# Four layers on 16 images of 28 x 28: one tile for all padded signs, and another order of VectorE's and ScalarE's steps where one layer ends and the next begins

## The chip, the cores and the metric

The kernel runs on one core of one Trainium2 chip. The metric is the device time of one execution in microseconds (us); for the kernel before it is 963.3 us, the median of three runs (963.19 to 964.45). TensorE is called PE in the profile, VectorE DVE, ScalarE ACT, GpSimd POOL and SyncE SP.

## What is computed

The input is a tensor of 16 images, 256 channels, 28 x 28 pixels, in fp32. Four layers follow each other:

```python
# layer 0: signs, 3x3 convolution with signs of weights, batch norm, residual
y = sat_conv2d(sign(x), sign(w)) * mean(abs(w));  x = bn_over_batch(y) * gamma + beta + x
# layer 1: per image, two branches with a squeeze-and-excite gate each
residual = prelu(x, a_alpha1)
y = prelu(bn(conv3x3(hardsign(x + a_move), clip(a_w))), a_alpha2)
y = bn(gate(mean(s * x + (1 - s) * y)) * y * residual) + residual
u = prelu(bn(conv1x1(hardsign(y + f_move), clip(f_w))), f_alpha2)
x = bn(gate(mean(s2 * y + (1 - s2) * u)) * u) + y
# layer 2: norm over the batch, signs, binary convolution, twice; norm; residual
o = prelu(binconv(sign(batchnorm(x)), w1), a1)
o = prelu(binconv(sign(batchnorm(o)), w2), a2)
x = prelu(batchnorm(o) + x, a3)
# layer 3: attention over the 784 pixels of an image, width 64
q, k, v = Wq x, Wk x, Wv x;  x = Wp softmax(q k / 8) v + x
```

The norms of layers 0 and 2 are over all images. So the next layer can't begin before the last image's statistics are there: these places are called borders here.

## The kernel before, in words

The channels lie on the 128 partitions in two groups (k = 0, 1). An image is 784 columns, and a matmul takes half of them (HN = 392), one bank of PSUM.

**Layer 0 and the two halves of layer 2** are `sign_layer` (L330 on). Its list of blocks says what is worked on at a time. For layer 0 the list is `whole_images(PARTS)`: IMAGES (L52) are taken whole, and the rest of PARTS follows: image 15 as one half and two quarters. For every block `products` issues the matmuls of L348 (18 for a half image, all into one tile of two PSUM banks), ScalarE writes the signs of the next image into `fpads`, `post` issues VectorE's statistics of the block before (L616, L1180), one or two weight steps follow, and `apart` splits the packed sums: ScalarE twice (L359, L360), VectorE once (L362). `fpads` is a tile for two images with a border of zeros, which POOL clears (`sign_pads`, L109). It is made once for layers 0 (in the space that layer 1 uses for `vs`) and once more for layer 2. Layer 1 has two such tiles of its own, `pads` (L493), which POOL clears in `constants` (L561).

**Border 0 to 1.** `norm` (L189) makes scale and shift from the statistics. ScalarE computes the two shifts (L213), `zb1` and `bi0`, in a row; `enter` (L685, VectorE) and `sign1` (L693, ScalarE) make image 0's signs, `transform` (L698, VectorE) the sums that the convolution L732 takes.

**Layer 1** is `iteration(b)` for 15 images, written so that the steps of three images interleave, and `last_iteration` for image 15. Its two convolution results of one parity are `conv_pair` with i = 0, 1: the two banks of one tile, read by `rows_out` (L771, VectorE, L777). After it, from L1060, come the last gates and the statistics for layer 2: `squares` (L883, ScalarE), `products` (L886, VectorE; both write a scrap tile "rn" of two buffers), `unit_u` (L865, ScalarE), `unit_b` (VectorE), the small steps L1079 to L1101, `gates`, a table load for the square root (L1105) and `sign_norm`. `keep_busy(n)` (L437) issues n matmuls on a tile of zeros whose result is not used.

**Border to attention.** After layer 2 `norm("l2c", ...)` gives `sg3` and `bg3` by VectorE alone, a dummy exponential loads its table (L1229), and `attend_unshifted` begins: for each half of image 0, `finish_a` (ScalarE: scale and shift, L1345), `finish_b` (VectorE: add and prelu, L1353 and L1354), `queries_keys` (PE, L1367). Then queries and keys are copied out of PSUM (L1374, L1378) and the scores (L1390) begin.

**The end.** For the last image the denominators (L1411) are inverted (L1437), watched by ScalarE (L1612, L1615), the values copied (L1617) and multiplied (L1441), projected (L1471) and added (L1480, L1482), and stored in two parts from ScalarE's queue (L1503). `raise_flag` (L1495) sums up the watched numbers and sets `flag`, which every engine loads at the end (L1258) to decide whether a careful second run of all is needed.

Within `tc.manual_schedule(engines=...)` the named engines run their instructions in the order of the program; outside it a scheduler orders them. Waits are set by the framework from the tiles that are read and written.

Of the kernel before, what the change touches and what calls it, by code (L numbers as in the profile page):

```python
# [27 lines left out]
F32 = mybir.dt.float32  # L28
# [22 lines left out]
NB = len(PARTS)  # L51
IMAGES = [(i, 0, S) for i in range(B - 1)]  # L52
EARLY = 22
# [30 lines left out]
def forward(ctx: ExitStack, tc: tile.TileContext, d: dict, out: bass.AP, careful: bool):  # L84
# [24 lines left out]
    def sign_pads(pool, tag):  # L109

        t = pool.tile([P, 2, 2, S + 2, S + 2], SIGNS, tag=tag, name="fpads")
        for i in (0, S + 1):
            for edge in (t[:, :, :, i:i + 1, :], t[:, :, :, :, i:i + 1]):
                nc.gpsimd.memset(edge.bitcast(F32) if careful else edge, 0.0)
        return t
# [72 lines left out]

    def norm(name, moments, gamma, beta, sf=None, then=lambda r: None, shifts=()):  # L189


        half, e = vtile(name + "_half"), vtile(name + "_e")
        V.tensor_scalar(half, gamma, -0.5, None, ALU.mult)
        if sf is not None:

            tt(e, sf, sf, ALU.mult)
            V.tensor_scalar(e, e, 1e-30, 1.0 / EPS, ALU.max, ALU.mult)
            V.reciprocal(e, e)
        m, var = moments()
        v, c, less = vtile(name + "_v"), vtile(name + "_c"), vtile(name + "_less") if shifts else None  # L200
        if sf is not None:
            tt(v, var, e, ALU.add)
        else:
            V.tensor_scalar(v, var, EPS, None, ALU.add)
        r = rsqrt(name, v, half, (lambda: V.tensor_scalar(less, m, -1.0, None, ALU.mult)) if shifts else None)
        then(r)
        if not shifts:
            tt(c, m, r, ALU.mult)
            return r, tt(c, beta, c, ALU.subtract)
        cs = [vtile(f"{name}_c{i}") for i in range(len(shifts))]  # L210
        for o, b in zip(cs, shifts):
            for k in range(2):
                A.activation(o[:, k:k + 1], r[:, k:k + 1], AF.Identity, bias=b[:, k:k + 1], scale=less[:, k:k + 1])  # L213
        return r, *cs

# [213 lines left out]
    with tc.tile_pool(name="ps_conv", bufs=3, space=PSUM) as psc, \  # L429
# [13 lines left out]
        with tc.tile_pool(name="ph1", bufs=1) as ph:  # L443

            fpads = sign_pads(ph, "vs")
            xs, ns = [None] * B, [None] * B
# [45 lines left out]

            pads = [const.tile([P, 2, S + 2, S + 2], BF16, tag=f"pad{i}", name=f"pad{i}") for i in range(2)]  # L493

# [60 lines left out]

            moved = vtile("moved")

            def constants():
                tt(moved, pv("b0"), pv("a_move"), ALU.add)
                for p in pads:  # L560
                    nc.gpsimd.memset(p, 0.0)  # L561
# [9 lines left out]
                for i, bn in enumerate(bns):  # L571
# [3 lines left out]
                    tt(c_bn[:, two], bn[:, 1::4], c_bn[:, two], ALU.subtract)  # L575
                tt(cc, c2, c4, ALU.add)

                for o, q in ((ra1, "a_alpha1"), (ra2, "a_alpha2"), (rf2, "f_alpha2")):
# [166 lines left out]
            def conv_pair(b, mo, i, u, parts=range(2)):  # L745
                if i == 0 and 0 in parts:
                    pairs[b, mo, u > 0 and u < 3] = conv_ps()
                conv(b, mo, u, pairs[b, mo, u > 0 and u < 3][:, i, :HN], parts)

            def first_pair():  # L750
                ps = pairs[0, 0, True] = conv_ps()
                for part in range(2):
                    for i, u in enumerate((1, 2)):
                        conv(0, 0, u, ps[:, i, :HN], (part,))
# [8 lines left out]
            def sum_pair_b(b, mo):  # L763
# [5 lines left out]
                pairs[b, mo] = uv  # L769

            def rows_out(b, mo, rows=range(2)):  # L771
                ps, uv = pairs[b, mo, False], pairs[b, mo]
                if 0 in rows:
                    ys[b, mo] = full("yu", f"y{b}_{mo}", 6)
                two = ys[b, mo].rearrange("p (a two b) -> p two a b", two=2, b=S)
                for i in rows:
                    V.scalar_tensor_tensor(  # L777
                        two[:, i], ps[:, i, :HN].rearrange("p (a b) -> p a b", b=S), us1[:, mo:mo + 1],
                        uv[:, i].rearrange("p (a b) -> p a b", b=S), ALU.mult, ALU.add,
                    )  # L780
# [195 lines left out]
            def last_iteration(b):  # L976
# [32 lines left out]
                px = hidden_x(B, TWO)  # L1009
                conv_pair(b, 1, 0, 0, (0,))  # L1010
                h = hidden_a(B, px, TWO)
                sum_pair_b(b, 1)
                h = hidden_b(B, h, TWO)
                conv_pair(b, 1, 0, 0, (1,))
                rows_out(b, 1, (0,))
                g = gates(h, some=TWO)
                conv_pair(b, 1, 1, 3)
                branch2(b - 1, 0, g[:, 1])
# [14 lines left out]
            with tc.manual_schedule(engines={ET.PE, ET.DVE, ET.Activation}):  # L1033
                sc0, zb1, bi0 = norm("l0", mom, pv("g0"), pv("b0"), sf0, first, (moved, pv("b0")))
                mom.doubt(doubts[:, 0:2 * NB])
                sign1(0, 0)
                enter(0, 1, sc0)
                sign1(0, 1)
                for k in range(2):
                    for u in (1, 2):  # L1040
                        transform(0, u, k)
# [31 lines left out]
                squares(x2[b][:, 0, :], shift[:, 0:1], sum_vv[:, 0:1])  # L1073
                for i, v in ((b, sum_vv[:, 1:2]), (b - 1, sum_sq[:, 1, b - 1:b])):
                    products(x2[i][:, 1, :], shift[:, 1:2], x2[i][:, 1, :], v)

                last = wpool.tile([P, 2, N], F32, tag="wa", name="last")
                px = hidden_x(B + 1, TWO)
                V.tensor_reduce(m1, sum_x2[:, :, 0:B - 1], AX.X, ALU.add)  # L1079
                tt(m1, m1, sv, ALU.add)  # L1080
                V.scalar_tensor_tensor(without_g[:, 0], m1, 1.0 / (B * N), shift, ALU.mult, ALU.add)
                unit_u(b, 0, last[:, 0, :])
                unit_b(b, 0)
                tt(d1, sv, sum_x2[:, :, b - 1], ALU.add)
                V.scalar_tensor_tensor(d1, shift, 2.0 * N, d1, ALU.mult, ALU.add)
                V.scalar_tensor_tensor(
                    sum_vv[:, 1:2], d1[:, 1:2], shift[:, 1:2], sum_vv[:, 1:2], ALU.mult, ALU.add
                )
                unit_u(b, 1, last[:, 1, :])
                unit_b(b, 1)  # L1090
# [3 lines left out]
                h = hidden_b(B + 1, hidden_a(B + 1, px, TWO), TWO)  # L1094
                for k in range(2):
                    products(x2[b][:, k, :], shift[:, k:k + 1], us[b, k], sum_uv[:, k:k + 1])
                V.tensor_scalar(of_g[:, 0], su, 1.0 / (B * N), None, ALU.mult)
                V.tensor_scalar(without_g[:, 1], sum_uv, 2.0 / (B * N), None, ALU.mult)
                V.tensor_reduce(v1, sum_sq[:, :, 0:B - 1], AX.X, ALU.add)
                tt(v1, v1, sum_vv, ALU.add)  # L1100
                V.tensor_scalar(v1, v1, 1.0 / (B * N), EPS, ALU.mult, ALU.add)  # L1101
                g = gates(h, dqg[:, 2], TWO)
                keep_busy(14)

# [21 lines left out]
        with tc.tile_pool(name="ph2", bufs=1) as ph:  # L1126
            if careful:
                w2b = packed_weights(ph, tag="wb")
            fpads = sign_pads(ph, "fpads")

# [93 lines left out]

            keep_busy(45)
            sg3, bg3 = norm("l2c", mom, pv("g3"), pv("b3"), sf2)
            tt(bg3, bg3, cc, ALU.add)

            A.activation(small.tile([P, 2], F32, tag="mv", name="e"), sg3, AF.Exp, scale=0.0)  # L1229

# [70 lines left out]
def attend_unshifted(ctx, tc, d, out, wqk, wv, wp, keys, worst, doubts, flag, pv, finish):  # L1301
# [126 lines left out]
    def denominators(b):  # L1428

        dns[b] = two_banks(pssc, "sc")[:, 0, :HN] if b == B - 1 else one_bank(pssm, "sm")  # L1430

# [76 lines left out]
    with tc.manual_schedule(engines={ET.PE, ET.Activation, ET.DVE, ET.Pool}):  # L1508

        ps = [two_banks(psmi, "mi"), two_banks(pssc, "sc")]  # L1510
        for h in range(2):
            n = slice(h * HN, h * HN + HN)
            finish_a(0, n)
            finish_b(0, n)
            queries_keys(0, h, ps[h])
        keep_busy(8)
        for h in range(2):
# [83 lines left out]
        for c in range(3):  # L1601
            values(b, c)
        denominators(b)
        for c in range(3, NC_):
# [6 lines left out]
        junk = buf("junk", 1, shape=(P, HN))  # L1611
        A.activation(junk, dns[b], AF.Copy, accum_out=watched[0])  # L1612
        for n in parts:
            invert(b, n)
        A.activation(junk[:, parts[0]], r[:, parts[0]], AF.Copy, accum_out=watched[1])  # L1615
        V.tensor_reduce(watched[2], r[:, parts[1]], AX.X, ALU.add)
        A.copy(os[b][0], avs[b][:, :HN])  # L1617
        up = raise_flag(two_banks(psmi, "mi")[:, 0, :])
        for n in parts:
            normalize(b, n)  # L1620
        up()

# [4 lines left out]
                (parts[1], 0, [one_bank(pssm, "sm"), one_bank(psav, "av")]),  # L1627
                (parts[1], 1, two_banks(pssc, "sc")),
            )
        ]  # L1630
        for add in adds[0::2]:
            add()
        store(b, slice(0, 1), nc.scalar)
        for add in adds[1::2]:
            add()
# [179 lines left out]
```

## Time and profile before

| | |
|---|---|
| device time, median of 3 (lowest, highest) | 963.3 us (963.19, 964.45) |
| profiled execution: its own time, its span | 963.05 us, 961.3 us |
| mean granted TensorE clock | 0.998 |
| layer 0, last real matmul ends | about 107.7 us |
| layer 1, first matmul | 114.95 us |
| layer 2, first matmul of its two halves | 468.52, 573.68 us |
| first scores of the attention | 686.83 us |
| last store issued, end | about 956, 961.3 us |
| DMA, mean | 110 GB/s |

All times are from the start of the span. The profile gives, for each engine, when an instruction began and how long it took, and for idle time what ended it. The chain that ended last is followed back from the last instruction through what released each step. An average share of busy time says little here; the borders are short and have limits of their own, so they are read in the timeline.

### The profile page before, as it was taken

How to read it: one execution, taken by the hardware profiler on the slowest of the kernel's cores; microseconds unless marked ns; L12 is line 12 of the kernel's file. 1: busy time of each engine (PE TensorE's matmuls, PEld its weight loads, DVE VectorE, ACT ScalarE, POOL GpSimd, SP SyncE). 2: the span in 40 equal slices, each digit the busy share in tenths (PEclk: the TensorE clock that was granted, in tenths of full speed). 3: DMA queues.
4: the chain of work that ended last, by engine and by line, in shares of the span. 5: the costliest groups of instructions: out<-in, count | busy, mean ns of one | idle time of the engine just before them, and what ended most of it. 6: DMA issues, size and time to landing. Idle time of an engine off the chain costs nothing.

```text
span 961.3 us, 14808 instructions
## 1 busy us (share of the span) xinstructions
PE 942.2 (98%) x5613; PEld 578.4 (60%) x5619; DVE 773.4 (80%) x1424; ACT 719.0 (75%) x1200; POOL 140.9 (15%) x149
## 2 busy tenths in 40 slices
PE   8999999999999999999999999999999999999995
PEld 4555577787778778776555555555444444444442
DVE  3777798999988888977799988999666868777765
ACT  6887768888887888865788868888666666676652
POOL 3001100000000000000100000000145353444431
PEclk9999999999999999999999999999999999999999
DMA  9978512444433233101670000000043443425212
GB/s 344 347 272 287 198 34 84 147 141 149 146 103 101 101 134 110 42 35 67 239 297 1 1 1 2 1 1 1 14 81 75 89 114 79 123 72 131 67 68 105
DMA packets 26948, 105.82 MB, mean 110 GB/s; under 512 B 3490, under 2 KB 7268, under 8 KB 26868
## 3 DMA queue, kind: packets, MB, share of 16 engines
q1 hardware_dynamic: 20948, 73.44, 21.5%
q0 software_dynamic: 5632, 30.54, 11.7%
q8 instruction: 46, 0.75, 0.3%
q10 hardware_dynamic: 288, 0.80, 0.2%
q14 instruction: 34, 0.28, 0.1%
HBM read 72.67 MB, written 32.11 MB: 109 GB/s over the span
## 4 chain that ended last, share of the span: by engine, by line
PE 84%; DVE 9%; ACT 3%; issue 1%; DMA 1%; SPq 1%; DVEq 0%; ACTq 0%
PE cv L732 29%; PE cv L348 22%; PE sc L1390 8%; PE av L1411 8%; PE cv L852 4%; PE mi L1367 4%; DVE p L1178 2%; PE sm L1453 2%; PE mi L1471 2%; PE sm L1411 1%; DVE ab L362 1%; DMA xs<-in_x_dram 1%; DVE l2c_fin L1180 1%; DVE l2b_fin L1180 1%; PE hid L642 1%
## 5 line engine op out<-in xcount | busy, mean ns | idle before, releaser
L348 PE MATMUL cv<-fpads,wpk 128*128 128x392 f16 (+1 forms) x1746 | 295.3, 331 | 2.1 <-DVE wpk L275 1.1
L732 PE MATMUL cv<-vs,w 128*128 128x392 bf16 (+1 forms) x1536 | 285.8, 355 | 1.8 <-DVE vs L134 1.4
L348 PEld LDWEIGHTS <-wpk 128*128 128x128 f16 x1746 | 169.3, 97 | 128.7 <-issue 3.0
L732 PEld LDWEIGHTS cv<-vs,w 128*128 128x128 f32 x768 | 142.0, 190 | 10.7
L1394 ACT ACTIVATE es<-sc 128x784 f32<-128x784 f32 x112 | 87.3, 822 | 41.4 <-PE sc L1390 41.4
L732 PEld LDWEIGHTS <-w 128*128 128x128 f16 x768 | 66.3, 99 | 56.7 <-issue 17.7
L1390 PE MATMUL sc<-q,keyswa 64*128 64x392 f32 x448 | 89.9, 513 | 0.9 <-ACT es L1394 0.9
L359 ACT ACTIVATE t<-cv,rounding 128x392 f32<-128x392 f32 (+2 forms) x82 | 51.9, 633 | 41.4 <-PE cv L348 41.4
L1178 DVE SCALAR_TENSOR_TENSOR p<-ab,vec 128x392 f32<-128x392 f32 x128 | 79.1, 618 | 2.3
L1411 PE MATMUL av<-es,v 128*64 128x392 f32 x448 | 80.7, 499 | 0.0
L1404 POOL TENSOR_TENSOR sum<-sum,es 128x784 f32<-128x784 f32 x32 | 67.2, 2100 | 3.1 <-ACT es L1394 0.7
L1390 PEld LDWEIGHTS sc<-q,keyswa 64*128 64x128 f32 x448 | 38.9, 186 | 44.0 <-issue 17.1
L1378 DVE COPY keyswa<-mi 64x392 f32<-64x392 f32 x31 | 16.3, 565 | 52.7 <-ACT q L1374 52.7
L880 POOL DMA_DIRECT2D x2d<-x x16 | 8.6, 537 | 336.7 <-DVE x L874 276.1
L1411 PEld LDWEIGHTS av<-es,v 128*64 128x64 f32 x448 | 29.4, 136 | 47.4 <-issue 47.0
L714 ACT CAST vs<-vs 128x840 fp32r<-128x840 bf16 x63 | 54.1, 883 | 2.9 <-DVE vs L134 2.9
L852 PE MATMUL cv<-z,fw 128*128 128x392 f32 x256 | 48.6, 341 | 0.1
L362 DVE SCALAR_TENSOR_TENSOR ab<-ab,cv 128x392 f32<-128x392 f32 x64 | 35.4, 553 | 16.4 <-ACT ab L360 16.4
L852 PEld LDWEIGHTS cv<-z,fw 128*128 128x128 f32 x256 | 45.9, 188 | 1.0 <-ACT z L844 0.9
L1367 PE MATMUL mi<-p,wqk 128*128 128x392 f32 x124 | 45.1, 506 | 0.1
L1402 POOL TENSOR_TENSOR sum<-es 128x784 f32<-128x784 f32 x16 | 30.0, 1876 | 91.0 <-ACT es L1394 91.0
L441 PE MATMUL unused<-idle 128*128 128x512 bf16 x166 | 39.6, 394 | 3.2 <-POOL idle L477 3.0
(290 smaller groups left out, 1502.9 us busy)
## 6 DMA issues: line engine op xcount, KB each, us to landing
xs<-in_x_dram SPq DMA_DIRECT2D x30, 784.0 KB, 5.9
x2d<-x POOLq DMA_DIRECT2D x16, 784.0 KB, 3.6
out_dram<-p SPq DMA_DIRECT2D x15, 784.0 KB, 3.7
p<-x2d POOLq DMA_DIRECT2D x14, 784.0 KB, 6.8
p<-x2d SPq DMA_DIRECT2D x13, 784.0 KB, 15.3
n0d<-n POOLq DMA_DIRECT2D x16, 392.0 KB, 5.6
n<-n0d SPq DMA_DIRECT2D x16, 392.0 KB, 3.2
st<-in_w_dram SPq DMA_DIRECT2D x12, 384.0 KB, 6.5
```

Of the source, the lines that this page charges most:

```text
L348: T.matmul(pss[j][:, n // size if careful else h, :rows * S].rearrange("p (a b) -> p a b", b=S), lhsT=w[:, n, t, :], rhs=pads[:, blocks[j] ...
L359: A.activation(by_halves(t, blocks[j]), ps, AF.Identity, bias=rounding, scale=1.0 / PACK)
L362: V.scalar_tensor_tensor(a, b, -PACK, ps, ALU.mult, ALU.add)
L714: copy(v, w)
L732: T.matmul(ps.rearrange("p (a b) -> p a b", b=S), lhsT=w[:, k, c, u, mo * P:(mo + 1) * P], rhs=v[:, b % 2, u, k, :, c:c + S], start=((part ...
L852: T.matmul(ps[:, h, :HN], lhsT=w[:, k, mo * P:(mo + 1) * P], rhs=z2[b][:, k, h * HN:(h + 1) * HN], start=(k + i == 0), stop=(k + i == 2),)
L1178: V.scalar_tensor_tensor(p, y, alpha[:, mo:mo + 1], y, ALU.mult, ALU.max)
L1367: T.matmul(ps[:, h, :HN], lhsT=wqk[:, k, :], rhs=x[b][:, k, h * HN:(h + 1) * HN], start=(k == 0), stop=(k == 1))
L1390: T.matmul(ps[:, h, :HN], lhsT=chunk[rows], rhs=qs[b][rows], start=True, stop=True)
L1394: A.activation(e, ps[:, :, :HN], AF.Exp, scale=0.125)
L1404: (V if late else nc.gpsimd).tensor_tensor(sums[b, late], sums[b, late], e, ALU.add)
L1411: T.matmul(ps[64 * h:64 * h + 64, :HN], lhsT=w, rhs=e[:, h, :], start=start, stop=stop)
```

## The change

Six edits. (1) Layer 0 takes images 0 to 13 whole and image 14 as two halves. (2) `fpads` is made once, in the pool of constants, for layers 0 and 2, and `pads` are its two halves, read as bf16; the clearing of `pads` and of the second `fpads` falls away. (3) `norm` with `late` returns a function that makes a shift when it is called: at border 0 to 1 `bi0` comes behind the signs of image 0; at the border to attention ScalarE makes `bg3` with `b3c` (b3 + cc, made at the start in `constants`). (4) In `last_iteration` the results for i = 0 and 1 have a tile each; the steps after layer 1 stand in another order, and 9 dummies in place of 14. (5) At the border to attention channels 128 to 255 of image 0 are scaled and added in one VectorE step, then shifted by ScalarE; the table of the exponential is loaded behind the two `queries_keys`; 39 dummies in place of 45. (6) At the end ScalarE's watching stands behind the inversions and the copy, the flag behind the first add, with its matmul in the free bank of the denominators' tile.

```diff
-IMAGES = [(i, 0, S) for i in range(B - 1)]
+IMAGES = [(i, 0, S) for i in range(B - 2)]
...
-            pads = [const.tile([P, 2, S + 2, S + 2], BF16, tag=f"pad{i}", name=f"pad{i}") for i in range(2)]
+            pads = [
+                const.tile([P, 2, S + 2, S + 2], BF16, tag=f"pad{i}", name=f"pad{i}") if careful
+                else fpads[:, i].bitcast(BF16) for i in range(2)
+            ]
...
+            def conv_alone(b, mo, i, u, parts=range(2)):
+                if 0 in parts:
+                    alone[i] = conv_ps()
+                conv(b, mo, u, alone[i][:, i, :HN], parts)
...
-                conv_pair(b, 1, 1, 3)
+                conv_alone(b, 1, 1, 3)
...
-                sc0, zb1, bi0 = norm("l0", mom, pv("g0"), pv("b0"), sf0, first, (moved, pv("b0")))
+                sc0, shift0 = norm("l0", mom, pv("g0"), pv("b0"), sf0, first, True)
+                zb1 = shift0(moved)
                 mom.doubt(doubts[:, 0:2 * NB])
                 sign1(0, 0)
                 enter(0, 1, sc0)
                 sign1(0, 1)
+                bi0 = shift0(pv("b0"))
...
-                for i, v in ((b, sum_vv[:, 1:2]), (b - 1, sum_sq[:, 1, b - 1:b])):
-                    products(x2[i][:, 1, :], shift[:, 1:2], x2[i][:, 1, :], v)
+                products(x2[b][:, 1, :], shift[:, 1:2], x2[b][:, 1, :], sum_vv[:, 1:2])
                 last = wpool.tile([P, 2, N], F32, tag="wa", name="last")
+                V.tensor_reduce(m1, sum_x2[:, :, 0:B - 1], AX.X, ALU.add)
+                tt(d1, sv, sum_x2[:, :, b - 1], ALU.add)
+                tt(m1, m1, sv, ALU.add)
+                V.scalar_tensor_tensor(d1, shift, 2.0 * N, d1, ALU.mult, ALU.add)
                 px = hidden_x(B + 1, TWO)
...
+                products(x2[b - 1][:, 1, :], shift[:, 1:2], x2[b - 1][:, 1, :], sum_sq[:, 1, b - 1:b])
                 unit_u(b, 0, last[:, 0, :])
                 unit_b(b, 0)
+                V.tensor_reduce(v1, sum_sq[:, :, 0:B - 1], AX.X, ALU.add)
...
+                tt(v1, v1, sum_vv, ALU.add)
                 V.tensor_scalar(of_g[:, 0], su, 1.0 / (B * N), None, ALU.mult)
+                products(x2[b][:, 0, :], shift[:, 0:1], us[b, 0], sum_uv[:, 0:1])
+                V.tensor_scalar(v1, v1, 1.0 / (B * N), EPS, ALU.mult, ALU.add)
+                products(x2[b][:, 1, :], shift[:, 1:2], us[b, 1], sum_uv[:, 1:2])
+                g = gates(h, dqg[:, 2], TWO)
                 V.tensor_scalar(without_g[:, 1], sum_uv, 2.0 / (B * N), None, ALU.mult)
...
-                keep_busy(14)
+                keep_busy(9)
...
-            keep_busy(45)
-            sg3, bg3 = norm("l2c", mom, pv("g3"), pv("b3"), sf2)
-            tt(bg3, bg3, cc, ALU.add)
-
-            A.activation(small.tile([P, 2], F32, tag="mv", name="e"), sg3, AF.Exp, scale=0.0)
+                keep_busy(39)
+                with tc.manual_schedule(engines={ET.DVE, ET.Activation}):
+                    sg3, shift3 = norm("l2c", mom, pv("g3"), pv("b3"), sf2, late=True)
+                    bg3 = shift3(b3c)
...
-        for h in range(2):
-            n = slice(h * HN, h * HN + HN)
-            finish_a(0, n)
-            finish_b(0, n)
+        for n in cuts:
+            v = x[0][:, 1, n]
+            V.scalar_tensor_tensor(v, v, sg3[:, 1:2], x2[0][:, 1, n], ALU.mult, ALU.add)
+        for h, n in enumerate(cuts):
+            finish_a(0, n, (0,))
+            v, w = (x[0][:, k, n] for k in range(2))
+            A.activation(w, w, AF.Identity, bias=bg3[:, 1:2])
+            V.tensor_tensor(v, v, x2[0][:, 0, n], ALU.add)
+            for k, y in enumerate((v, w)):
+                V.scalar_tensor_tensor(y, y, alpha[:, k:k + 1], y, ALU.mult, ALU.max)
             queries_keys(0, h, ps[h])
+        A.activation(ph.tile([P, 2], F32, name="e"), sg3, AF.Exp, scale=0.0)
...
+        last = two_banks(pssc, "sc")
         denominators(b)
...
-        A.activation(junk, dns[b], AF.Copy, accum_out=watched[0])
         for n in parts:
             invert(b, n)
-        A.activation(junk[:, parts[0]], r[:, parts[0]], AF.Copy, accum_out=watched[1])
         V.tensor_reduce(watched[2], r[:, parts[1]], AX.X, ALU.add)
         A.copy(os[b][0], avs[b][:, :HN])
-        up = raise_flag(two_banks(psmi, "mi")[:, 0, :])
+        A.activation(junk, dns[b], AF.Copy, accum_out=watched[0])
+        A.activation(junk[:, parts[0]], r[:, parts[0]], AF.Copy, accum_out=watched[1])
         for n in parts:
             normalize(b, n)
-        up()
...
-        for add in adds[0::2]:
-            add()
+        adds[0]()
+        up = raise_flag(last[:, 1, :])
+        adds.append(project(b, 1, two_banks(psmi, "mi"), parts[1]))
+        adds[2]()
         store(b, slice(0, 1), nc.scalar)
+        up()
```

## The prediction

> **What bounds the kernel now.** I read the page first: busy shares, then the chain that ended last, by engine.
>
> ```profile
> PE 942.2 (98%) x5613; PEld 578.4 (60%) x5619; DVE 773.4 (80%) x1424; ACT 719.0 (75%) x1200; POOL 140.9 (15%) x149
> PE 84%; DVE 9%; ACT 3%; issue 1%; DMA 1%; SPq 1%; DVEq 0%; ACTq 0%
> ```
>
> TensorE (PE) is the bound, but its 98% counts dummy matmuls (`keep_busy`). The 12% of the chain on VectorE and ScalarE is the start, the borders between layers and the end. Inside the layers PE runs without a hole (a layer-1 iteration takes 21.0 us), so only borders can give time, and what a border gives stays: everything after it moves with it. So I read the timeline at each border; columns: start, duration, instruction, idle before and releaser. First layer 0 to layer 1:
>
> ```profile
> 101.74 0.90 ACT L359 ACTIVATE t<-cv,rounding 128x784 f32<-128x784 f32 x1
> 103.65 0.97 DVE L362 SCALAR_TENSOR_TENSOR n<-n,cv 128x784 int16<-128x784 int16 x1 [1.98 <-ACT n L360]
> 109.67 0.63 DVE L616 BATCH_NORM_STATS2 l_fin<-n 128x6 f32<-128x196 int16 x2
> 113.53 1.83 ACT L694 ACTIVATE pad<-xs,l_c 128x784 bf16<-128x784 f32 x2
> 115.82 2.45 PE L732 MATMUL cv<-vs,w 128*128 128x392 bf16 x13 [0.20 <-DVE vs L134]
> ```
>
> VectorE idles 1.98 us for whole image 14, then runs behind until 110.30. Second, the end of layer 1:
>
> ```profile
> 447.06 2.34 PE L732 MATMUL cv<-vs,w 128*128 128x392 bf16 x12 [0.38 <-DVE y L777]
> 458.04 1.03 DVE L886 SCALAR_TENSOR_TENSOR product<-x,shift 128x784 f32<-128x784 f32 x1 [0.87 <-ACT square L883]
> 464.21 1.28 ACT L1105 ACT_TABLE_LOAD   x1
> 464.96 0.51 DVE L134 TENSOR_TENSOR dqg<-gates,s_bn 128x2 f32<-128x2 f32 x1
> 466.51 0.20 ACT L230 ACTIVATE l2a_t<-l_v 128x2 f32<-128x2 f32 x1 [0.79 <-DVE l_v L134]
> ```
>
> Third, layer 2 to attention; fourth, the end:
>
> ```profile
> 678.51 0.16 DVE L134 TENSOR_TENSOR l2c_c<-l2c_c,cc 128x2 f32<-128x2 f32 x1
> 678.70 2.53 ACT L1345 ACTIVATE p<-p,l2c_c,l2c_r 128x392 f32<-128x392 f32 x4
> 684.15 0.93 PE L1367 MATMUL sc<-p,wqk 128*128 128x392 f32 x2 [0.21 <-DVE p L1354]
> ...
> 948.20 2.62 DVE L1437 RECIPROCAL r<-sc 128x196 f32<-128x196 f32 x2 [2.36 <-ACT junk L1612]
> 952.19 0.14 DVE L1500 TENSOR_SCALAR flag<-mi 1x1 int32<-1x1 f32 x1
> 954.29 1.03 DVE L1482 TENSOR_TENSOR p<-sc,p 128x392 f32<-128x392 f32 x2
> ```
>
> **Part by part.** *Image 14 by halves.* Its first half leaves PE 3.07 us before the whole (half of 6.14). ScalarE is free for it at 99.95 (after L523), so t and n of the half end at 101.1 (0.59+0.62, pitch 0.53), and VectorE's L362 (0.56) and two statistics (0.98) run in its old idle. The four L527 (1.45) follow to 104.1, the second half to 105.65, `sf0` to 105.95, image 15's first half to 107.5, its first quarter to 108.5; the last quarter is ready at 108.62 as before and ends at 109.62 (0.34+0.63). That is 110.30 - 109.62 = 0.67 us earlier. Cost: ScalarE pays 2.42 for 1.84 and VectorE 1.12 for 0.97, hidden in idle before 104.60; uncovered, 0.7. Bounds 0.3 (half-grown queue) to 0.7. Image 14's store is queued on POOL behind the second half, 104.66 instead of 104.62; SP's reload of image 0 waits for it, lands at 111.26, and is wanted at 111.64: 0.38 of cover. `bi0`'s two ScalarE steps (0.65) move behind sign1: sign1 starts when VectorE is done (113.37), not at 113.53, so -0.16; behind them on ScalarE only the widening waits (115.2 against a need at 116.7, shifted times). Sum **-0.83**.
>
> *conv_alone.* The matmul of 447.06 waited 0.38 for VectorE's read of the same tile's other bank. In a tile of its own it waits only for its slot; a slot left by unit_u has been free since 442.5. VectorE, idle 1.20 before its next rows_out, follows. **-0.38** (bounds 0 and 0.38).
>
> *Layer 1's last steps.* The second product waited 0.87 for ScalarE's square (its buffer); seven small steps (0.07 to 0.2 each) fill that hole and leave the tail. unit_b then follows ScalarE at 459.19 and 460.61 instead of 459.55 and 461.03. The dummies before `hid` still end at 462.58, so the gates come no sooner. Of the two last products the second ends at 464.24 for 464.36, but behind it stand one step instead of five, and POOL's four fpads memsets (1.82 from 464.56), beside which `dqg` took 0.51 where its like take 0.16, are gone. l_t comes at 464.44 instead of 465.52. ScalarE's table load and root end at 465.71, so the root of the variance starts at 465.75 for 466.51: **-0.76** (bounds 0.4 and 1.1). The dummies (15 for 20, at 0.22 us each) still end 0.4 us before the first sign.
>
> *One set of signs.* Pads and fpads in one tile: two memsets at the start (3.49 us on POOL) and four at layer 2 go. The start is set by image 1's load (PE at 15.70), so nothing beyond the 0.5 just counted. Sign1 and the transforms touch the same halves in the same order as before: 0. `b3c` adds 0.16 on VectorE at about 24 us, beside matmuls: 0.
>
> *Layer 2 to attention.* The three steps for the shift (0.59 from 678.12) become two on ScalarE (0.58), beside which VectorE starts on channels 128 to 255 with scale and add in one step (0.63). ScalarE then has four steps of 0.63 from 678.70 (ends 679.37, 679.96, 680.6, 681.25). VectorE: add 679.40, prelu 680.63, prelu 681.2; second half add 681.74, prelus 682.4 and 682.96. The last key before ended at 684.10, so PE's last projection starts 1.14 earlier, if ScalarE can copy: the Exp table load (1.28) plus one step (0.2) now stands from 681.27 to 682.77, ahead of the copies. First-half copies end at 683.75, the second half is out of PE at 683.97. Nothing lost. Here the row and a rule part: the load and the next step are 1.30 apart in the trace (464.21 and 465.51), while the Trainium skill's "ScalarE: Activation LUTs" (What ACT_TABLE_LOAD costs) puts a switch at 1.28 plus a drain of 1.38. By the rule the copies would end 1.1 later and this border would give 0.1. I take the row: **-1.14** (bounds 0.1 and 1.2).
>
> *Fewer dummies* (45 to 39, 14 to 9). Granted clock at the emptiest stretch of the trace:
>
> ```profile
> 951.00:953.00 2.00, 0.72 (x8) 0.64 (x10) 1.19 (x6) 0.00 (x0) 0.00 (x0) 1.00 0.00 0
> 280.08:301.08 21.00, 21.00 (x121) 16.63 (x120) 18.56 (x39) 17.79 (x28) 0.53 (x1) 1.00 0.35 115
> ```
>
> PE was 0.72 of 2 us busy and the clock stayed 1.00. "TensorE: Matmul & The Clock Gate" (Part 1) halves the clock after an idle window of about 3.4 us, which speaks against shorter dummies; by it a hole of that length would cost, as an estimate, half a window (1.7 us) at each of the two borders. The new holes are 0.4 us, so I take 0.
>
> *The end.* The reciprocals waited for ScalarE's reading of the same bank; now they start when PE is done, 947.52 for 948.20. One reduce and then both normalizes (951.27 for 952.26, held by ScalarE's copy at 950.64), then the adds; the flag's three VectorE steps and its matmul (PE waits for `ok` at 952.65, with the last projection behind it) stand between adds. The last add ends at 954.35 for 955.32: stores 0.97 earlier. But the flag comes at 953.3 for 952.33, and every engine loads it before it can branch. POOL's rows at the end:
>
> ```profile
> L1258 POOLq TENSOR_LOAD <-flag x1: 488/488/488, 952.4 to 952.4; - x1
> L1810 POOLq DRAIN  x1: 3903/3903/3903, 955.0 to 955.0; - x1
> ```
>
> POOL's drain ended at 958.9 and the last barrier began at 960.5, 0.8 before the end. Moved by 1.0 it ends at 959.9, and the span 0.8 later: a gain of 0.6. If the drain was waiting for the stores, the gain is 0.97. I take **-0.70**, nearer the drain's row.
>
> Sum: 0.83 + 0.38 + 0.76 + 1.14 + 0.70 = 3.81. The profiled execution took 963.05 (span 961.3): 959.24. The median is 0.25 above it: **959.5**.
>
> **Rivals.** (1) *One border gives nothing*: the table switch costs the page's 2.66, or image 0's reload lands after its cover of 0.38, or the drain eats the end. Total 2.2 to 2.8: about 960.6. For it: covers of 0.2 to 0.4 us at three places. Against: each is a row above. (2) *New waits take the old ones' places at most borders* (the new tile's slot is not the free one, VectorE's order falls back behind ScalarE): 1 us is left, 962.3, no change to be measured. (3) *Slower*: a pad is now a slice 3600 bytes into a tile. If VectorE's transforms of odd images lose their speed there (589 ns for 840 bf16 elements, against 954 for 784 fp32, so about 1.02 us), each odd image costs 4 x 0.43 = 1.7 us of VectorE; eight of them 13.8, so 973 if all of it reaches PE. It decides once more than 0.7 us of each 1.7 reaches PE. Against: VectorE has 2.4 us free in an iteration (18.56 of 21.0), and rows of 60 bytes already start at every such offset. (4) *More*: the end gives its 0.97 and layer 1's tail 1.1: 958.4.
>
> **Numbers.** Likeliest (0.67): 958.6 to 960.2. (4) 0.07, below that. (1) 0.17, 960.2 to 961.3. (2) 0.06. (3) 0.03. The range 958.2 to 961.3 leaves out about 0.12. A measurement tells 0.2% (1.9 us) from no change: faster (below 961.4) 0.91, same 0.06, slower 0.03.
>
> **What would show it.** The last L616 of layer 0 ends near 109.6; no wait of PE on y L777; the first layer-2 matmul at 466.5 in place of 468.52 (0.83 + 1.14 earlier); first scores at 683.7 (3.1 earlier than 686.83); transforms still 589 ns; the last store 4.1 earlier than 955.3, POOL's drain starting only 2 to 2.2 earlier. Wrong if a border's shift is missing at the next border, above all if ScalarE's copies of keys wait behind the table load.

## The result, and the profile after

The changed kernel takes 959.88 us (median of 6 runs, 958.58 to 961.03) beside 964.05 for the kernel before on the same chip (6 runs, 963.19 to 965.05): a ratio of 0.9956, 95% interval 0.9943 to 0.9969. Timed again later it took 959.12 (6 runs, 958.83 to 962.66) beside 963.84 (11 runs): 0.996, interval 0.9947 to 0.9973. Its profiled execution took 959.34 us with a span of 957.6, against the 959.24 that the prediction's sum gave (959.5 for the median). So the total was met; several of its terms were not, and that is what the rest is about.

The page of the changed kernel, busy shares and chain:

```profile
PE 939.1 (98%) x5602; PEld 577.3 (60%) x5608; DVE 772.4 (81%) x1424; ACT 719.9 (75%) x1204; POOL 136.7 (14%) x143
PE 87%; DVE 7%; ACT 3%; issue 1%; DMA 1%; SPq 1%; DVEq 0%; ACTq 0%
```

The borders shrink on the chain (VectorE 9% to 7%). To see where, I cut both spans at the same matmuls. Each stretch runs from the start of one matmul to that of another of the same number in TensorE's order, so it can be compared from kernel to kernel (us):

| stretch | before | after | gain | predicted |
|---|---|---|---|---|
| start to layer 0's continuous work | 15.70 | 15.85 | -0.15 | 0 |
| to layer 1's first convolution from the second channel group (layer 0 and border 0 to 1) | 100.13 | 99.68 | 0.45 | 0.83 |
| layer 1's loop, to the last iteration | 325.50 | 324.94 | 0.56 | 0 |
| to the last `conv(.., 1, 1, 3)` (`conv_alone`) | 5.74 | 5.21 | 0.53 | 0.38 |
| to the last 1x1 convolution | 9.11 | 9.09 | 0.02 | 0 |
| to layer 2 (layer 1's last steps) | 12.36 | 11.19 | 1.17 | 0.76 |
| layer 2's first half, to the first matmul of its second | 105.16 | 105.17 | -0.01 | 0 |
| to the first scores (layer 2's second half and border to attention) | 113.15 | 112.05 | 1.10 | 1.14 |
| to the last denominators | 258.50 | 258.52 | -0.02 | 0 |
| to the end | 15.94 | 15.86 | 0.08 | 0.70 |
| span | 961.28 | 957.56 | 3.72 | 3.81 |

The timeline of the changed kernel at border 0 to 1 (start, duration, instruction, idle before; line numbers are those of the changed kernel, L367 being the old L362, L625 the old L616, L703 the old L694, L741 the old L732):

```profile
101.37 0.56 DVE L367 SCALAR_TENSOR_TENSOR n<-n,cv 128x392 int16<-128x392 int16 x1 [0.87 <-ACT n L365]
106.22 0.16 DVE L134 TENSOR_TENSOR l_e<-sf 128x2 f32<-128x2 f32 x1
107.00 0.16 DVE L198 RECIPROCAL l_e<-l_e 128x2 f32<-128x2 f32 x1
109.37 0.63 DVE L625 BATCH_NORM_STATS2 l_fin<-n 128x6 f32<-128x196 int16 x2
115.53 1.88 PE L741 MATMUL cv<-vs,w 128*128 128x392 bf16 x10 [0.28 <-DVE vs L134]
```

VectorE's idle of 1.98 is down to 0.87, but the last statistics end at 110.00 and not at 109.62. The end of layer 1:

```profile
445.68 1.56 PE L741 MATMUL cv<-vs,w 128*128 128x392 bf16 x8
462.68 1.28 ACT L1123 ACT_TABLE_LOAD   x1
462.69 0.16 DVE L134 TENSOR_TENSOR dqg<-gates,s_bn 128x2 f32<-128x2 f32 x1
464.08 0.19 ACT L235 ACTIVATE l2a_t<-l_v 128x2 f32<-128x2 f32 x1
```

The convolution has no wait in front; `dqg` takes 0.16 for 0.51; the root of the variance waits for nothing but the table. The border to attention and the end:

```profile
678.50 1.28 ACT L1546 ACT_TABLE_LOAD   x1
680.01 0.48 ACT L1401 COPY keyswa<-mi 64x392 f32<-64x392 f32 x1
683.18 0.93 PE L1413 MATMUL sc<-q,keyswa 64*128 64x392 f32 x4
...
943.89 2.62 DVE L1460 RECIPROCAL r<-sc 128x196 f32<-128x196 f32 x2 [1.68 <-PE sc L1434]
949.46 0.13 DVE L1523 TENSOR_SCALAR flag<-sc 1x1 int32<-1x1 f32 x1
949.99 0.54 DVE L1505 TENSOR_TENSOR p<-mi,p 128x392 f32<-128x392 f32 x1
```

The first copy of keys starts 1.51 after the table load began, with the dummy exponential between. At the end the last add is over at 950.53, 8.83 after the last denominators began (before: 955.32 - 945.33 = 9.99). So the stores go 1.16 earlier, and yet the end comes only 0.08 earlier.

### The profile page after: what moved, and what is told of

It is laid out like the page before. It is cut to its first block, busy times and chain, and to the rows that moved or that the text cites. A ratio compares the mean times of both kernels' runs of the same rounds, so it can differ in the third digit from the quotient of the medians.

```text
span 957.6 us, 14783 instructions
## 1 busy us (share of the span) xinstructions
PE 939.1 (98%) x5602; PEld 577.3 (60%) x5608; DVE 772.4 (81%) x1424; ACT 719.9 (75%) x1204; POOL 136.7 (14%) x143
## 3 DMA queue, kind: packets, MB, share of 16 engines
q0 software_dynamic: 5632, 30.54, 11.9%
## 4 chain that ended last, share of the span: by engine, by line
PE 87%; DVE 7%; ACT 3%; issue 1%; DMA 1%; SPq 1%; DVEq 0%; ACTq 0%
PE cv L741 29%; PE cv L353 23%; PE sc L1413 9%; PE av L1434 8%; PE cv L868 5%; PE mi L1390 5%; PE sm L1476 2%; DVE p L1197 2%; PE mi L1494 2%; PE sm L1434 1%; DVE ab L367 1%; DMA xs<-in_x_dram 1%; DVE l2b_fin L1199 1%; PE gate L836 1%; PE hid L651 1%
## 5 line engine op out<-in xcount | busy, mean ns | idle before, releaser
L741 PE MATMUL cv<-vs,w 128*128 128x392 bf16 (+1 forms) x1536 | 285.2, 354 | 1.0 <-DVE vs L134 1.0
L741 PEld LDWEIGHTS cv<-vs,w 128*128 128x128 f32 x768 | 141.7, 190 | 10.5
L741 PEld LDWEIGHTS <-w 128*128 128x128 f16 x768 | 66.3, 99 | 55.6 <-issue 17.1
L367 DVE SCALAR_TENSOR_TENSOR ab<-ab,cv 128x392 f32<-128x392 f32 x64 | 35.4, 553 | 16.2 <-ACT ab L365 16.2
L1460 DVE RECIPROCAL r<-sm 128x392 f32<-128x392 f32 x15 | 39.1, 2608 | 3.4 <-PE sm L1434 3.0
```

Source lines behind the costliest of these rows:

```text
L367: V.scalar_tensor_tensor(a, b, -PACK, ps, ALU.mult, ALU.add)
L741: T.matmul(ps.rearrange("p (a b) -> p a b", b=S), lhsT=w[:, k, c, u, mo * P:(mo + 1) * P], rhs=v[:, b % 2, u, k, :, c:c + S], start=((part ...
```

## The experiments

In the texts on record "the fetch" is the loading of the instructions that follow the branch at the program's end.

**The end undone (e1).** Edit 6 put back (cut).

```diff
-        last = two_banks(pssc, "sc")
         denominators(b)
...
+        A.activation(junk, dns[b], AF.Copy, accum_out=watched[0])
         for n in parts:
             invert(b, n)
```

> The changed kernel with its last edit alone undone (order of the watch copies, the denominators' banks, the flag's place and the last projection's banks as before). Read: the stretch from the start of the last denominators to the end of the span, 15.97 us before and 15.90 after the change. The prediction's theory (the new order lets the two stores go 0.7 to 1.0 us earlier and the end follows): 16.6 to 16.9 here only if something else in the change costs that much, and else 15.97; so it needs another cost of the change in the end. Theory of the fetch: the stores go about 1.1 us later than in the changed kernel but land within about 3.7 us of issue instead of 4.7, so that the stretch is 15.9 to 16.0: the edit at the end is worth under 0.1 us.

Measured: 16.22 from the last denominators to the end. Neither theory's number. The stretch varies from profile to profile: the three kernels with the old order (before, e1, e6) have 15.94, 16.22 and 15.99, mean 16.05; the seven with the new one and the branch (after, e3, e4, e7, e9, e10, e11) 15.59 to 15.86, mean 15.71. The edit is worth about 0.34. But this run took 963.13, 3.4 us of it at a place that the edit doesn't touch: 101.51 at border 0 to 1 and 326.53 in layer 1's loop. More on that below.

**No branch at the end (e2, e5).** The changed kernel and the one before without the conditional careful pass.

```diff
-    again = forward(tc, d, out, False)
-    with tc.If(again > 0):
-        forward(tc, d, out, True)
+    forward(tc, d, out, False)
```

> The changed kernel without the conditional second, careful forward pass behind its end: what is left out is the repair of doubtful signs; the first pass, its flag and its stores are computed as they are. Theory of the fetch: in the changed kernel the five engines take the branch at 950.2 to 951.9, just as the last store is issued (950.57), and the instructions fetched for what follows use the same DMA engines as the store, which lands 4.7 us after its issue. Without the branch it lands about 3.1 to 3.7 us after issue and the stretch from the last denominators to the end falls from 15.90 to 14.3 to 14.9. Rival (the store itself is slow there: its position, or ScalarE's queue): landing stays at 4.7 and the stretch falls by nothing or only by what the wait for the flag took.

> The kernel before without the conditional careful pass behind its end (what is left out is the repair of doubtful signs). Read: the stretch from the last denominators to the end, 15.94 us before, 15.86 after the change, 12.99 for the changed kernel without the branch. Theory (the change of the end does move both stores by 1.15 us, and the code fetched behind the branch takes most of it back): about 14.1 here, so that without the branch the edit is worth 1.1. Rival (the edit is worth no more than it is with the branch, 0.1 to 0.4): 13.1 to 13.4.

Measured from the start of the last denominators (issue: ScalarE's second store; landed: when SyncE's wait for that store's semaphore ended):

| kernel | last store issued | landed | end |
|---|---|---|---|
| before | 10.01 | 13.68 | 15.94 |
| e1, old order | 10.03 | 13.52 | 16.22 |
| after | 8.87 | 13.60 | 15.86 |
| e3, new order | 8.87 | 13.39 | 15.65 |
| e8, new order, flag earlier | 8.84 | 13.25 | 15.51 |
| e5, before, no branch | 10.86 | 13.35 | 14.71 |
| e2, after, no branch | 8.87 | 11.63 | 12.99 |

With the branch the store lands at 13.25 to 13.68 whether it is issued at 8.87 or at 10.03; without it, 2.5 to 2.8 after its issue. The queues of the last stretch show what is gone, first the changed kernel, then e2 (queue 14 holds instructions: packets, MB, share; then issue to landing, median of the two stores):

```profile
q14 instruction: 8, 0.07, 1.8%
out_dram<-p ACTq DMA_DIRECT2D x2, 392.0 KB, 2.8
```

```profile
q14 instruction: 1, 0.01, 0.1%
out_dram<-p ACTq DMA_DIRECT2D x2, 392.0 KB, 2.5
```

The trace has the landing of this store in 16 parts (times from the last denominators): in e2 15 are in by 11.31 and the last at 11.61; in the changed kernel 11 are in by 11.33 and the other five come at 12.31 to 13.58, while code is loaded from 9.91 to 15.38. So the fetch holds the last parts of the store back, by 2.0 us in the changed kernel (4.73 less 2.76) and by 1.2 in the old order (3.67 less 2.49); the theory is right in kind and too small in size for e2 (12.99 for 14.3 to 14.9), since SyncE's last waits after the landing shrink as well (1.36 for 2.26). For e5 it missed by 0.6: there the stores are issued 0.85 later than in the kernel before, because TensorE's granted clock fell to 0.50 at 952.43 (more on that below) and the last group of the projection's matmuls took 0.93 for 0.53. Without the branch the edit gives 1.72, of which 0.85 is that delay; 0.87 is the edit's.

**Image 14 whole (e3, and timed as e10).**

```diff
-IMAGES = [(i, 0, S) for i in range(B - 2)]
+IMAGES = [(i, 0, S) for i in range(B - 1)]
```

> The changed kernel with image 14 of layer 0 whole again. Read: the stretch from layer 0's first continuous matmul to the first convolution of layer 1 for the second half of the channels, 100.12 us before and 99.68 after. Theory: all of that gain is image 14's halves, so 100.05 to 100.15 here. Rival (prediction): a part of it, 0.16, is the bias of the second sign step set behind the first sign: then 99.95.

Measured: 100.15 (100.14 in e10), before 100.13. The halves give 0.47 and `bi0`'s new place gives nothing.

**Signs apart, signs shared alone, and one tile moved (e4, e6, e7).** e4 is the changed kernel with edit 2 undone; e6 the kernel before with edit 2 alone; e7 the changed kernel with one tag claimed early, so that `vs` lies where it lay before:

```diff
             fpads = sign_pads(ph, "vs") if careful else sign_pads(const, None)
+            if not careful:
+                ph.tile([P, 2, 4, 2, HR, S + 2], FR, tag="vs", name="vs_place")
```

> The changed kernel with separate padded signs for each layer again (and GpSimd's memsets of their borders with them). Read two stretches. First layer 1's loop, from its first convolution to the last iteration, 325.50 before and 324.93 after. Theory A (the shared pads make the pace: what was GpSimd's memsets or the place of the pads in SBUF): back to 325.5. Rival (another edit, or the code's layout): stays 324.9. Second, from the last iteration's one-by-one convolution to layer 2's first, 12.35 before and 11.19 after. Theory B (GpSimd's memset for layer 2's pads ran beside VectorE's small steps there and made one of 0.16 us take 0.51): 11.55 to 11.7. Rival (only the new order of the steps counts there): 11.2.

> The kernel before with one part of the change alone, the one set of padded signs. Read layer 1's loop, 325.50 us before, 324.94 after, 325.49 for the changed kernel with the signs apart: the sharing, alone, should give 324.9 if it makes the pace; 325.5 if it only does so together with another edit. And the stretch from the last one-by-one convolution of layer 1 to layer 2's first, 12.36 before, 11.19 after, 11.31 for the changed kernel with the signs apart. Theory (in the old order three single-input steps of VectorE, of 0.16 to 0.17 elsewhere, take 0.45 to 0.58 because GpSimd's memset of 0.63 runs then; no memset, no stall): 11.9. Rival (only the order counts): 12.2 to 12.4.

> The changed kernel, with nothing but the place of one tile in SBUF changed: the transformed signs of layer 1, 26,880 bytes a partition, which TensorE reads there in two thirds of the kernel's first half, stand first in their pool again as they did before the change. Read layer 1's loop, 324.94 us with shared signs and 325.49 with them apart. Theory of the place (the sharing changed only where tiles lie): 325.5. Rival (it is the sharing itself: other bytes written and read, GpSimd's work): 324.9.

Layer 1's loop: 325.49 with the signs apart, 324.94 with edit 2 alone, 325.50 with edit 2 and the tile in its old place. So the cause is where tiles lie in SBUF, and not the sharing itself. It need not be `vs`: with its tag claimed first, all later tiles of that pool move too, among them the weights `w1` that the same matmuls read. The groups of TensorE within the loop show where the time is, first e7, then the changed kernel:

```profile
L743 PE MATMUL cv<-vs,w 128*128 128x392 f32 x750 | 179.3, 375 | 0.0
```

```profile
L741 PE MATMUL cv<-vs,w 128*128 128x392 f32 x750 | 178.7, 374 | 0.0
```

One ns in each of 750 matmuls with fp32 operands, 0.6 us in all; the bf16 ones on `vs16` have 334 in both. Which tile counts, and what of its place, no run tells.

Layer 1's last steps: 11.31 with the signs apart, so sharing them gives 0.12 behind the new order, and the order alone 1.05; with edit 2 alone 12.00, so 0.36 in the old order, near the 11.9 that e6's theory gave. Theory B (11.55 to 11.7 in e4) fell: a memset on GpSimd doesn't slow every small step of VectorE. The rows of the kernel before:

```profile
464.56 1.82 POOL L114 MEMSET fpads<- 128x120 f16 x4 [11.25 <-DVE product L886]
464.88 0.58 DVE L1101 TENSOR_SCALAR l_v<-l_v 128x2 f32<-128x2 f32 x1
465.03 0.45 DVE L221 TENSOR_SCALAR l2a_hb<-vec 128x2 f32<-128x2 f32 x1
```

The same memsets in e4:

```profile
465.15 1.83 POOL L114 MEMSET fpads<- 128x120 f16 x4 [11.05 <-DVE dqg L134]
465.33 0.16 DVE L134 TENSOR_TENSOR dqg<-l_t,without_g 128x4 f32<-128x4 f32 x1
```

Before, the step with one input at 464.88, `dqg` behind it and the next all end at 465.46 to 465.48, just after the second memset's end (465.44). In e4 no one-input TENSOR_SCALAR starts during a memset: the new order has put them ahead. The steps with two inputs that run beside the memsets take 0.16, and so does a reciprocal, with one input, inside the last memset (0.17 at 466.49). The Trainium skill ("SBUF — State Buffer", two separate sides) has a rule that fits: a VectorE step in a mode that uses both ports and a GpSimd step lock a shared pair of ports for the whole instruction, and a VectorE step with two inputs is locked out only by a GpSimd step that reads SBUF. That the TENSOR_SCALAR steps here use such a mode, and the reciprocal doesn't, no run shows.

**Why some runs are 3 us longer (e8, e9, e11, e12).** In e1, e2 and e12 border 0 to 1 took 101.3 to 102.0 and the loop of layer 1 326.4 to 326.5. The timeline of e1 at that border:

```profile
110.06 6.11 SPq L461 DMA_DIRECT2D n<-n0d  x3
113.82 1.03 DVE L697 SCALAR_TENSOR_TENSOR xs<-n,l_r,xs 128x784 f32<-128x784 int16 x1 [1.88 <-DMA n<-n0d]
116.37 0.68 PE L741 MATMUL cv<-vs,w 128*128 128x392 bf16 x3 [2.54 <-DVE vs L134]
```

SyncE's reload of image 0 (L461) is issued at 110.06, in the changed kernel's own profile at 108.60. It waits for the write-back of image 14, from whose buffer it needs the room: issued by GpSimd at 105.11 and 105.15, landed 4.8 later here and 3.3 later there. VectorE then waits 1.88. That makes TensorE's hole 2.54 instead of 0.70, and the clock falls. Columns behind the window: its length, busy time of PE, PEld, DVE, ACT and POOL, granted clock, DMA share, GB/s; e1, then the changed kernel:

```profile
118.00:122.00 4.00, 4.00 (x16) 3.01 (x15) 1.90 (x6) 3.33 (x5) 0.00 (x0) 0.63 0.06 23
```

```profile
118.00:122.00 4.00, 4.00 (x23) 3.05 (x23) 2.35 (x3) 2.46 (x3) 0.00 (x0) 1.00 0.00 0
```

16 matmuls for 23 in 4 us: 1.6 us on top of the 1.83 of the border.

The record of the granted clock in the traces tells more. Within each of the 14 profiles the clock changes only at times that lie a whole number of 3.41 us apart (e1: up at 8.30, down at 117.53, up at 120.94, down at 957.21). So it looks as if it were set window by window, on a grid that lies elsewhere in each run. TensorE's busy time in a window (the ends of matmuls are modelled), and the clock in the next:

| profile | window | busy of 3.41 us | clock in the next |
|---|---|---|---|
| e1, border 0 to 1 | 114.12 to 117.53 | 0.89 | 0.50 |
| e12, border 0 to 1 | 113.48 to 116.89 | 1.06 | 0.50 |
| e5, end | 949.02 to 952.43 | 1.23 | 0.50 |
| e6, end | 949.29 to 952.70 | 1.23 | 0.50 |
| e2, border 0 to 1 | 115.09 to 118.50 | 1.28 | 0.50 |
| e4, start | 7.51 to 10.92 | 1.39 | 0.50 |
| e11, start | 7.06 to 10.47 | 1.65 | 0.50 |
| e6, start | 7.21 to 10.62 | 1.71 | 1.00 |
| before, end | 950.62 to 954.03 | 1.75 | 1.00 |
| after, end | 947.41 to 950.82 | 1.99 | 1.00 |

Two of these pairs as the profile has them, e11's start and e5's end:

```profile
7.06:10.47 3.41, 1.65 (x8) 0.62 (x8) 0.56 (x1) 2.81 (x5) 0.00 (x0) 1.00 1.00 364
10.47:13.88 3.41, 3.41 (x12) 1.63 (x11) 1.67 (x3) 2.68 (x4) 0.00 (x0) 0.50 1.05 408
```

```profile
949.02:952.43 3.41, 1.23 (x10) 0.48 (x8) 2.86 (x8) 0.94 (x3) 0.00 (x0) 1.00 0.00 2
952.43:955.84 3.41, 2.57 (x16) 2.05 (x14) 2.10 (x5) 0.00 (x0) 0.00 (x0) 0.50 0.00 0
```

In these traces the clock fell from 1.00 behind every window in which TensorE was busy for less than half of the time, and behind no other. It rose again behind windows with 3.14 to 3.41 us of work, at the low clock; behind 2.57 in e5 it did not. The length of a hole alone does not decide: 1.21 us at e11's start were followed by 0.50, 1.27 at e6's start by 1.00.

Of nine profiles with the halves three have the late reload, of the five without none; that is too few to say that the halves are the cause. What is seen is that with the halves SyncE's load of `fw` (256 KB) and eight small loads behind it are issued 1.3 us later, counted from the start of layer 0's continuous work (103.15 - 15.85 = 87.30, in e3 101.49 - 15.48 = 86.01), up against the reload. I tried to take the write-back off the path:

```diff
-                if r0 + rows == S:
+                if b == B - 2 and not careful:
+                    part = slice(r0 * S, (r0 + rows) * S)
+                    nc.gpsimd.dma_start(out=n0d[b][:, :, part], in_=ns[b][:, :, part])
+                elif r0 + rows == S:
                     nc.gpsimd.dma_start(out=n0d[b], in_=ns[b])
```

> The changed kernel with two edits of my own: at the end the flag's steps set ahead (the watch on the reciprocals before the copy, the flag straight behind the first add), and image 14 of layer 0 written back to DRAM half by half, so that the reload of image 0, which waits for that buffer, no longer hangs on one late write. First stretch, layer 0's start to layer 1's first convolution: 99.68 us, where two of four kernels with the halves showed 101.5 and 102.0 because the reload landed late. If my reading of the late write-back is right, SyncE issues the reload by 108.3 instead of 108.6 to 110.1. Second, the last denominators to the end, 15.64 to 15.86 in the changed kernel: theory of the fetch 15.2 to 15.5 (the branch is taken 0.6 earlier, the fetch is past when the stores go); rival (the stores fall into the fetch again) 15.7 to 16.0.

> The changed kernel once more, timed beside three others: of the five kernels with image 14 by halves that have separate profiles and the late fw load, two had the reload of image 0 landed late, at 1.8 to 2.3 us on the border and 1.55 more on layer 1's loop at a lower clock (about 3.4 in all). Theory (the changed kernel meets it in some runs): its times spread over 2 to 3.5 us, from about 958.6 up to 962, with a median near 959.9. Rival (those two were other code and the changed kernel does not meet it): within 1 us.

> The changed kernel with image 14 whole, timed. The late reload should be rarer or gone, as the fw load is issued 1.5 us earlier there and SyncE reads on sooner: theory: no slower in the median than the changed kernel although its border is 0.47 longer, 959.2 to 959.9, and a narrower spread. Rival (the halves are worth their 0.47 in every run): 0.3 to 0.5 slower in the median.

> The changed kernel with image 14 written back half by half and nothing else. Theory (the late write-back is what spreads the times): the upper runs go, median 959.0 to 959.4, spread under 1.2 us. Rival: as the changed kernel, 959.9 with its spread.

> Both of my edits, timed: the two writes and the earlier flag. From the one profile (956.85 span, the end 15.51 where the changed kernel has 15.64 to 15.86): median 958.6 to 959.1, 0.2 to 0.4 under the two writes alone; ratio to the kernel before 0.9945 to 0.995. Rival (landing differs from run to run by more than the flag brings): the same as the two writes alone.

| kernel | median | lowest, highest | ratio to before, 95% interval |
|---|---|---|---|
| e9, changed kernel | 959.12 | 958.83, 962.66 | 0.996 (0.9947, 0.9973) |
| e10, image 14 whole | 959.58 | 959.13, 959.79 | 0.9957 (0.9944, 0.997) |
| e11, two writes | 960.23 | 958.80, 961.61 | 0.9963 (0.995, 0.9976) |
| e12, two writes, flag earlier | 960.66 | 959.61, 962.24 | 0.9965 (0.9952, 0.9978) |

e8's profile was nearly as hoped: the reload issued at 107.72, the end 15.51. With e12's 15.64 the ends lie between the two theories; against the mean of 15.71, the flag 0.57 earlier is worth about 0.13, less than the 0.27 by which the seven profiles with the same end differ. The timed runs of e11 and e12 went against the theory: the medians did not fall, and the spreads are 2.8 and 2.6 where it had under 1.2. e12's own profile has the late reload again, at 109.89, and again behind the write-back: the second half's was issued at 105.28 and landed at 109.76, 4.5 later. (One of SyncE's small loads ahead of the reload took 1.54 to issue instead of 0.42, but SyncE was through with them at 108.95.) In e1, e2 and e12 alike the reload is issued 0.13 to 0.15 after that landing, so two writes don't keep it from being late; why a write-back lands late is open.

In e9 five of six runs lie within 1.0 and one is 3.5 above the median, as a late reload would have it; that run has no trace. Image 14 whole was 0.46 slower in the median, as its rival said, and narrower, as its theory said (0.66 from lowest to highest in five runs, against 3.83 in six), but the intervals overlap, and one slow run in six against none in five shows no difference. A third buffer for `n` would free the reload altogether; it was not tried. None of the other three is measurably better than the change as it is. Not all of the spread is the reload: the start alone lay between 15.39 and 17.47 in the profiles. The two latest, e4 and e11 (by 1.6 and 1.2), are those with the clock at 0.50 there, and e11's profiled run, with nothing late at the border (99.67), is the one of median time, so e11's times are no clean test of the write-back.

## Why the prediction was right in sum, and where its steps failed

- **Image 14 by halves, -0.67: mis-sized, 0.47.** The step that failed is "`sf0` to 105.95, image 15's first half to 107.5": it leaves out the three steps of `l_e`, which stand in VectorE's queue ahead of and between image 15's (106.22, 106.42, 107.00 above). The last statistics end at 110.00 for the 109.62 forecast, of which 0.15 is the later start.
- **`bi0` behind sign1, -0.16: wrong.** The pace behind the norm is set by VectorE's second `enter` (112.98 to 114.01) with ScalarE's second sign behind it (114.11). ScalarE's first sign coming sooner doesn't help.
- **"0.38 of cover" for the reload: the cover was named, the danger under-priced.** The prediction moved image 14's store by 0.04 and took the time to its landing as fixed. It was 3.3 before, and 4.5 to 4.8 in e1, e2 and e12. Nor did it follow SyncE's queue, where the halves move nine loads by 1.3; whether these delay the landing is not shown. Rival (1), of which it is one form, put the total at 2.2 to 2.8 for 3.81, a loss of 1.0 to 1.6; where the cover failed it cost 3.1 to 3.8, as the clock falls too. Against such runs the edit's gain of 0.47 is worth nothing that the times show.
- **`conv_alone`, -0.38: right mechanism, 0.53.** The wait shown was 0.38; before, the convolution started 0.89 after the gate's matmul started, now 0.37.
- **Layer 1's last steps, -0.76: mis-sized, 1.17.** Moved by the 1.40 that lies between the two kernels at that place, the table load starts 0.13 earlier than before (the sum had it fixed), the root of the variance overlaps the dummy root (0.11 behind its start, where the sum had 0.24, after its end: 0.13), and the signs behind it come 0.12 sooner because POOL's memsets are gone (e4). The memsets were credited with the stall of `dqg`; rightly, but e4 shows that the new order alone removes it.
- **One set of signs, 0: wrong, 0.56.** This edit of tiles moved other tiles. The prediction asked only whether the pads' own readers keep their speed (its rival of 973 is refuted) and not where the other tiles go.
- **Layer 2 to attention, -1.14: right, 1.10.** The row (1.30) and not the skill's 2.66 ("ScalarE: Activation LUTs", What ACT_TABLE_LOAD costs) held: a copy of keys started 1.51 after the load began, behind the exponential.
- **Fewer dummies, 0: right, on evidence that was luck.** In no profile does the clock fall at the changed kernel's two places. But the row that the prediction rested on (0.72 of 2 us busy, clock 1.00) is from the window of 1.75 in the table above; e5 and e6 run the same instructions there, on another grid, and their clock fell. The skill's idle window ("TensorE: Matmul & The Clock Gate", Part 1, about 3.4 us) has the length right, but it need not be idle: 1.65 us of work in it did not keep the clock (e11). The prediction's estimate of half a window, 1.7, is near the 1.41 to 1.59 measured in layer 1's loop.
- **The end, -0.70: wrong, 0.08 in the pair and 0.34 over ten profiles.** The add and the flag moved as forecast (0.97 and 1.0 forecast, 1.16 and 0.89 measured). What failed is the step that both its readings share, "POOL's drain" or "the stores": that the end follows what moved. POOL's drain ended at 956.1, SyncE's waits behind the last store at 956.7, so the stores decided; but the last one landed no sooner, because the fetch behind the branch holds it (e2, e5).

So two terms fell short by 1.0 together (border and end), and three gave 1.1 more (the loop, `conv_alone`, the last steps). That 3.81 comes so near to 3.72 is luck: errors of 1.0 and 1.1 cancel.

## What to carry to other kernels

Follow a moved step through every queue that it passes, SyncE's and GpSimd's too, and price a failed cover with what it triggers: here a load late by 1.8 us opened a hole that also cost 1.6 of clock. Ask of the last transfer what loads beside it: here, with code behind a branch loading, a store issued 1.16 earlier brought the end forward by 0.34 in the mean. Where TensorE waits, count its busy time in any 3.4 us and not the hole alone: up to 1.65 us of work lost the clock here, 1.71 kept it. Compare several profiles before crediting an edit with half a microsecond: tiles that merely lie elsewhere gave 0.56.

## What the runs showed of the hardware

- The place of `vs` and of the tiles behind it in SBUF alone changes its fp32 matmuls from 375 to 374 ns, 0.56 us over layer 1 (e7 against the changed kernel), to 0.01 us the same in every profile of either place that had no late reload.
- With the branch at the end the last store lands 4.7 us after its issue, without it 2.8, and the branch as a whole costs 2.9 us in the changed kernel (15.86 to 12.99, e2). Five of the store's 16 parts are late, the others are not.
- The granted clock was 0.50 in the 3.41 us behind a window of 3.41 us with 0.89 to 1.65 us of work on TensorE (e1, e2, e4, e5, e6, e11, e12), and stayed at 1.00 behind windows with 1.71 or more. The windows lie on a grid of their own in each run, so the same instructions lost the clock in e5 and kept it in the kernel before.
- A one-input TENSOR_SCALAR of 0.16 to 0.17 us on VectorE took 0.58 beside a GpSimd memset, to just behind its end; two-input steps that started beside such memsets took 0.16 (e4).
